# Due dates shifted per stage and chunk in a planned four-layer kernel on one core

## The chip, the cores and the metric

The kernel runs on one core of a Trainium2 chip. The metric is the device time of one execution in microseconds (us). The engines are named as in the profile: PE (matmuls), PEld (its weight loads), DVE (VectorE), ACT (ScalarE), POOL (GpSimd) and SP (SyncE, which issues the DMAs).

## The reference, cut to what matters

The input is x with 32 images of 128 channels and 56 x 56 points, float32. Four layers follow each other; each works on the group-normalised x and adds its result to x:

```python
x = x + dynamic_conv(_gn(x))      # layer 0: pooled softmax mixes 4 channel matrices; then silu of 3 dilated depthwise convs
x = x + spline(_gn(x))            # layer 1: cubic B-spline with 10 coefficients, point by point
x = x + linear_attention(_gn(x))  # layer 2: 8 heads on 8x8 pooled cells, then a depthwise 3x3
x = x + mamba(_gn(x))             # layer 3: layer norm, gated selective scan over all 3136 points
```

The scan of layer 3 is the heart of it. It has 256 inner channels with 16 states each, and runs along the points:

```python
dA  = exp(delta[..., None] * A)
dBu = delta[..., None] * B_ssm[:, :, None, :] * xc[..., None]
h   = dA_t * h + dBu_t                 # step by step over the points
y   = einsum('bdn,bn->bd', h, C_t)
out = einsum('bld,cd->blc', (y + xc * D) * silu(z), out_proj_w)
```

## The kernel before, in words

An image's 3136 points are cut into 7 chunks of 448. The scan of one chunk is 16 steps. In each step ACT makes the decays (two `da` activations), PE spreads the B rows (`pb`), DVE multiplies (`db`) and runs the scan instruction (`h`), POOL multiplies by the C rows (`hc`), and every other step PE sums the products (`y`). At the end of a chunk DVE multiplies by the gate (`sz`), PE projects (`mm<-sz,outT`), DVE adds to the image (`xt<-xt,mm`), and SP stores.

Three images are in work at the same time. While image b is scanned ("scan"), the inputs of its next chunk are made ("next", and "gate" for the silu gate), layers 1 and 2 and the norm weights of image b+1 are worked through ("rest"), and layer 0 of image b+2 ("conv"). `images` writes all this down for 6 images, and a hardware loop runs that block 5 times; a block before it makes the first two images ready, and a block behind it scans the last two images.

The order is not the written one. The class `Plan` records each operation as a `Work` with an engine, what it reads and writes, a cost from a formula (`price`), and a step: the number of the scan step beside which it was written. `order` then gives each work a due date, from the back: its step times `STEP` (4.0), or earlier where something that needs it is due earlier. To that date the table `LEAD` adds a shift. `attempt` is a list scheduler: engine by engine it takes the ready work that can start first by the costs, and among those the one due first, from the steps at most `WINDOW` (10) ahead of the first one not done. It also chooses the buffers (five of tag "v", four of PSUM "mm", three `da`, three `h`). `issue` then writes the instructions in that order. So every instruction carries the line of `issue`, L500 in the profile, and the tiles' names tell it apart.

The shift is looked up under two names:

```python
for w in self.works:
    chunk = w.step % (NCH * STEPS) // STEPS
    w.due += LEAD.get(w.what, 0.0) + LEAD.get(f"{w.what.split()[0]} {chunk}", 0.0)
```

`w.what` is the kind of work: stage, engine, the tile written and the first one read ("next scalar cen mm"). The second name is the stage and the chunk, 0 to 6, of the image that is being scanned ("rest 5"). Before the change the table has no entry of the second form, so that look-up always gives 0. A positive shift makes a work due later. What decides between two ready works on an engine is

```python
late = at + 0.3 * (w.table is not None and w.table != table)
key = (max(late, free[e]), w.due, i)
```

so a date counts only between works that could start at the same time, above all on an engine that has a queue of ready works. Nothing in the plan forbids a change of activation tables on ACT (exp, ln and silu need different ones); a load stands in the program wherever two neighbours differ.

Of the kernel before, what the change touches and what calls it, by code (L numbers as in the profile page):

```python
# [79 lines left out]
READY = 12  # L80

LEAD = {
    "conv gpsimd att att": -19.5,
    "conv gpsimd attb att": 18,
    "conv gpsimd attr att": -19,
    "conv gpsimd pooled mv": 6.5,
    "conv gpsimd pooled pooled": -7.5,
    "conv gpsimd rs ve": 6,
    "conv gpsimd xt xt": 3,
    "conv scalar aggT mm": 4.5,  # L90
    "conv scalar att att": -10.5,
    "conv scalar g mm": -34.5,
    "conv scalar part dwT": -66,
    "conv scalar vv mv": -34.5,
    "conv sync padded yc": 15,
    "conv sync stack padded": 38,
    "conv sync xt x_dram": 30,
    "conv tensor mm aggT": 24,
    "conv tensor mm dsT": 6,
    "conv tensor mm fc1T": -24.5,  # L100
    "conv tensor mm gmat": -10.5,
    "conv tensor mm ident": 4.5,
    "conv vector aggb aggb": 30.5,
    "conv vector aggb attb": -12.5,
    "conv vector att mm": -6,
    "conv vector hid mm": -18.5,
    "conv vector mv st": -69.5,
    "conv vector mx att": -22,
    "conv vector mx mx": 43.5,
    "conv vector st xt": -123.5,  # L110
    "conv vector ve mm": -20.5,
    "gate scalar sz mm": -3.5,
    "gate tensor mm wzT": 17.5,
    "next gpsimd delta delta": -15,
    "next gpsimd du delta": -186,
    "next gpsimd rstd cen": -157,
    "next gpsimd xn rstd": -26.5,
    "next scalar cen mm": -444.5,
    "next scalar dbl mm": 1,
    "next scalar delta mm": -30.5,  # L120
    "next scalar du du": 2.5,
    "next scalar du mm": -75,
    "next scalar rstd mm": 9.5,
    "next scalar rstd rstd": 12,
    "next scalar sq mm": -29,
    "next scalar xc mm": 47.5,
    "next sync flat delta": 11,
    "next sync flat du": 27,
    "next tensor mm ctr": -0.5,
    "next tensor mm dtT": -134.5,  # L130
    "next tensor mm jmat": -152.5,
    "next tensor mm winT": -6,
    "rest gpsimd ab ve": -84,
    "rest gpsimd ind xt": 5,
    "rest gpsimd mcell mcell": 20.5,
    "rest gpsimd rs ve": -13.5,
    "rest gpsimd rstd cen": 8.5,
    "rest gpsimd xn": 39,
    "rest gpsimd xt xt": 2.5,
    "rest scalar cen mm": 1.5,  # L140
    "rest scalar ctr cen": 61,
    "rest scalar hats hats": -32,
    "rest scalar hats mm": 3.5,
    "rest scalar rstd mm": 2.5,
    "rest scalar rstd rstd": 18.5,
    "rest scalar sq mm": -10,
    "rest scalar top ab": 1,
    "rest scalar vv mv": 10.5,
    "rest scalar ws mm": -38,
    "rest scalar ws ws": 26.5,  # L150
    "rest sync padded yc": -35.5,
    "rest sync stack padded": -36,
    "rest tensor mm ctr": -24,
    "rest tensor mm gmat": -31,
    "rest tensor mm ident": 6.5,
    "rest tensor mm jmat": 2.5,
    "rest tensor mm wpT": -36.5,
    "rest tensor mm wqT": -4.5,
    "rest tensor mm ws": 10.5,
    "rest tensor mm wspl": -147.5,  # L160
    "rest tensor mm wv": -13.5,
    "rest vector ab mg": 31.5,
    "rest vector ab rs": -29,
    "rest vector bia bia": -8,
    "rest vector bia kneg": -15.5,
    "rest vector cb mm": -12,
    "rest vector cube sq": -6.5,
    "rest vector kb mm": -3,
    "rest vector mcell mg": -45,
    "rest vector mg mm": 16.5,  # L170
    "rest vector mv st": -13.5,
    "rest vector nm": 26,
    "rest vector nm mg": 39.5,
    "rest vector rden mm": 4.5,
    "rest vector rden rden": -3,
    "rest vector st xt": 82.5,
    "rest vector ve mm": -113.5,
    "rest vector ws mm": 12,
    "rest vector xt mm": 14,
    "rest vector xt xt": -4.5,  # L180
    "scan gpsimd hc h": 1.5,
    "scan gpsimd last h": -47.5,
    "scan gpsimd rep last": 83.5,
    "scan scalar cb mm": -114,
    "scan scalar da rep": 9,
    "scan sync out_dram xt": 7,
    "scan sync rep flat": -19.5,
    "scan tensor mm outT": 22,
    "scan tensor mm sel": 7.5,
    "scan tensor pb sel": -45,  # L190
    "scan tensor y ddiag": 12,
    "scan tensor y ids": 4.5,
    "scan vector db rep": -7.5,
    "scan vector h da": 42.5,
    "scan vector sz sz": 193,
    "scan vector xt xt": 40.5,
    "sync rep flat": 8,
}

GN_EPS = 1e-5  # L200
# [1383 lines left out]
```

## Time and profile before

| | us |
|---|---|
| median of 3 runs | 14355.79 (14342.31 to 14364.07) |
| the profiled execution | 14350.93 |
| its span, first to last instruction | 14349.1 |
| first scan instruction after the start | 425.5 |
| one turn of the loop, 6 images | 2613.6 to 2621.4 |
| an image in the middle of a turn | 428.5 to 431.9 |
| first image of a turn | 448.9 to 454.3 |
| the block behind the loop, 2 images | 822.0 |

The turns and images are measured between the starts of DVE's scan instructions: 16 in a chunk, 112 in an image. A chunk of a middle image takes, from chunk 0 to chunk 6, about 59, 62, 67.5, 67, 56, 59 and 60 us. At the end of a turn all engines run dry and start again, with about 12 us more in the last chunk and 15 us more in the first one; in the 14 us around one such end (5640 to 5654 us) PE's granted clock is 0.51 of full speed.

In the profile's tables a row of a stretch has the span, then for each engine its busy time and the number of its instructions in brackets, PE's granted clock, the share that the DMA engines were busy, and GB/s. A row of waits names the waiting engine and tile, the engine and tile that ended the wait, the sum in us, how often, and the longest. A row of a group has its count, the busy time, the mean duration in ns, and the idle time ahead of it.

### The profile page before, as it was taken

The numbers are of one execution on the slowest core, as the hardware profiler recorded it, in microseconds if no ns is written. First come the engines' busy times: TensorE is split into PE (matmuls) and PEld (weight loads), VectorE is DVE, ScalarE is ACT, GpSimd is POOL, SyncE is SP. The second block draws the span as 40 slices with busy tenths as digits, with TensorE's granted clock in tenths as the row PEclk, the third lists the DMA queues.
The fourth block names the chain that finished last, engine by engine and source line by source line (L and its number), as shares of the span: only waits on it lengthen the run. The fifth ranks groups of instructions, "written<-read, shape, count | busy, mean of one in ns | idle before, by whom it ended". The sixth has DMA issues, their size and how long they took to land. (4 is left out here: it accounts for less than half of the span.)

```text
span 14349.1 us, 308089 instructions
## 1 busy us (share of the span) xinstructions
PE 12973.7 (90%) x122016; PEld 4333.4 (30%) x122016; DVE 12525.2 (87%) x10849; ACT 12711.8 (89%) x19296; POOL 11326.6 (79%) x10150
## 2 busy tenths in 40 slices
PE   7899999989999998999999999999998999999886
PEld 2223333323333332333233333333332333332221
DVE  1799989889888898898999888998988898989899
ACT  4899999989999998999999889999998899999886
POOL 2688888878788887888888878888887788888777
PEclk8999999999999999999999999999999999999998
DMA  5566566556665565665665655666655656656443
GB/s 128 121 140 141 134 151 140 131 128 140 139 146 134 135 140 131 145 141 131 141 141 136 145 126 134 138 141 143 147 133 127 138 134 150 141 129 143 109 107 74
DMA packets 1135727, 1927.31 MB, mean 134 GB/s; under 512 B 96434, under 2 KB 1133874, under 8 KB 1134260
## 3 DMA queue, kind: packets, MB, share of 16 engines
q1 hardware_dynamic: 1134260, 1907.39, 58.3%
q8 instruction: 965, 15.81, 0.5%
q14 instruction: 502, 4.11, 0.1%
HBM read 1541.47 MB, written 365.54 MB: 133 GB/s over the span
## 5 line engine op out<-in xcount | busy, mean ns | idle before, releaser
L500 POOL TENSOR_TENSOR hc<-h,cb 128x896 f32<-128x896 f32 x3584 | 7541.5, 2107 | 497.0 <-DVE h L500 240.6
L500 DVE TENSOR_TENSOR_SCAN h<-da,db 128x904 f32<-128x904 f32 x3584 | 7288.5, 2034 | 548.4 <-ACT da L500 236.9
L500 ACT ACTIVATE da<-rep,alog 128x448 f32<-128x448 f32 x7168 | 4477.1, 674 | 989.7 <-DVE h L500 765.1
L500 DVE TENSOR_TENSOR db<-rep,pb 128x904 f32<-128x904 f32 x3584 | 3944.5, 1101 | 352.7 <-POOL rep L500 82.4
L500 ACT ACT_TABLE_LOAD x1849 | 2372.3, 1283 | 50.1 <-DVE h L500 13.8
L500 PE MATMUL y<-hc,ids 128*32 128x448 f32 x14336 | 2023.7, 552 | 344.2 <-POOL hc L500 340.1
L500 PE MATMUL pb<-dbl,sel 128*32 128x452 f32 x14336 | 1825.9, 571 | 340.3 <-DVE db L500 308.5
L500 POOL TENSOR_TENSOR xt<-xt,v 128x448 f32<-128x448 f32 x1344 | 1538.6, 1146 | 465.0 <-ACT v L500 325.3
L500 PE MATMUL mm<-stack,dsT 96*32 96x448 f32 x16128 | 1819.2, 559 | 69.9 <-ACT wide L500 33.8
L500 POOL COPY last<-h 128x2 f32<-128x2 f32 x3072 | 572.7, 187 | 1628.3 <-DVE h L500 1511.1
L500 PE MATMUL mm<-xn,winT 128*32 128x448 f32 x14336 | 1588.4, 559 | 71.6 <-POOL xn L500 55.8
L500 ACT ACTIVATE wide<-mm,bia 128x448 f32<-128x448 f32 x2688 | 1557.8, 657 | 20.3 <-PE mm L500 18.3
L500 ACT ACTIVATE wide<-wide,one,scl 128x1344 f32<-128x1344 f32 x896 | 1377.6, 1537 | 7.7
L500 PE MATMUL mm<-wide,wspl 128*32 128x448 f32 x12544 | 1307.7, 560 | 56.2 <-DVE xt L500 27.9
L500 PE MATMUL mm<-xt,ident 128*32 128x448 f32 x8960 | 1082.6, 544 | 89.7 <-ACT cb L500 28.4
L500 PEld LDWEIGHTS y<-hc,ids 128*32 128x32 f32 x14336 | 533.9, 111 | 1439.0 <-POOL hc L500 689.5
L500 PE MATMUL mm<-dbl,sel 128*32 128x448 f32 x7168 | 865.4, 543 | 67.1 <-ACT yc L500 38.5
L500 PEld LDWEIGHTS mm<-stack,dsT 96*32 96x32 f32 x16128 | 547.6, 111 | 1113.6 <-issue 874.8
L500 PEld LDWEIGHTS pb<-dbl,sel 128*32 128x32 f32 x14336 | 393.7, 110 | 1439.9 <-DVE db L500 1124.5
L500 PEld LDWEIGHTS mm<-xn,winT 128*32 128x32 f32 x14336 | 474.9, 112 | 994.2 <-issue 778.1
L500 PEld LDWEIGHTS mm<-wide,wspl 128*32 128x32 f32 x12544 | 434.5, 114 | 897.0 <-issue 700.4
L500 DVE BATCH_NORM_STATS2 st<-xt 128x6 f32<-128x448 f32 x896 | 541.0, 613 | 135.3 <-POOL xt L500 131.9
(178 smaller groups left out, 13564.0 us busy)
## 6 DMA issues: line engine op xcount, KB each, us to landing
rep<-flat SPq DMA_DIRECT2D x1792, 448.0 KB, 8.3
stack<-padded SPq DMA_DIRECT2D x2016, 246.5 KB, 6.5
stack<-padded SPq DMA_DIRECT2D x672, 228.5 KB, 4.3
flat<-delta SPq DMA_DIRECT2D x224, 448.0 KB, 2.6
flat<-du SPq DMA_DIRECT2D x224, 448.0 KB, 2.8
padded<-yc SPq DMA_DIRECT2D x224, 244.0 KB, 2.2
padded<-yc SPq DMA_DIRECT2D x256, 199.5 KB, 3.4
xt<-x_dram SPq DMA_DIRECT2D x224, 224.0 KB, 9.3
```

Of the source, the lines that this page charges most:

```text
L500: call.func(*map(self.bind, call.args), **{k: self.bind(v) for k, v in call.keywords.items()})
```

## The change

The table `LEAD` is replaced. It gets 28 entries of the form stage and chunk, and nearly all entries by kind of work have other values; a few kinds lose their entry or get one. Nothing else in the program differs, neither the look-up nor any operation. Cut to its core:

```diff
 LEAD = {
-    "conv gpsimd att att": -19.5,
...
-    "conv scalar part dwT": -66,
...
+    "conv 1": -1,
+    "conv 2": 1.5,
+    "conv 5": -10.5,
+    "conv 6": -3,
+    "conv gpsimd att att": -11.5,
...
-    "gate scalar sz mm": -3.5,
-    "gate tensor mm wzT": 17.5,
+    "gate 0": 9.5,
+    "gate 1": 2.5,
+    "gate 2": 16,
+    "gate 3": 15,
+    "gate 4": 24.5,
+    "gate 5": 201,
+    "gate 6": 26.5,
+    "gate scalar sz mm": -4.5,
+    "gate tensor mm wzT": 13.5,
...
-    "next gpsimd du delta": -186,
-    "next scalar cen mm": -444.5,
-    "next tensor mm dtT": -134.5,
+    "next 0": -1,
+    "next 1": -1.5,
+    "next 2": -1,
+    "next 3": -1,
+    "next 4": 1,
+    "next 5": 4.5,
+    "next 6": -2.5,
+    "next gpsimd du delta": -164,
+    "next scalar cen mm": -438.5,
+    "next tensor mm dtT": -44.5,
...
+    "rest 1": 0.5,
+    "rest 2": 0.5,
+    "rest 3": -2.5,
+    "rest 4": 4.5,
+    "rest 5": 11.5,
+    "rest 6": 21.5,
...
-    "scan scalar cb mm": -114,
-    "scan vector sz sz": 193,
+    "scan 0": 0.5,
+    "scan 2": 3.5,
+    "scan 4": 5,
+    "scan 5": 20.5,
+    "scan scalar cb mm": -140.5,
+    "scan vector sz sz": 159,
...
 }
```

The dates decide the order, and the order decides the buffers and the places of ACT's table loads; so in the built program, by a comparison engine by engine, a good part of the instructions of the loop stand at another place in their queue or use another buffer of the same tag, and ACT has 349 table loads in a turn of the loop where it had 347. The block before the loop and the one behind it keep their number of them.

More of the change, by code (lines that the diff above doesn't have):

```diff
@@ L82 @@
 LEAD = {
-    "conv gpsimd att att": -19.5,
[L84 to L92, printed above, removed]
-    "conv scalar part dwT": -66,
[L94 to L97, printed above, removed]
@@ L98 @@
-    "conv tensor mm aggT": 24,
[L99 to L111, printed above, removed]
-    "gate scalar sz mm": -3.5,
@@ L113 @@
-    "gate tensor mm wzT": 17.5,
-    "next gpsimd delta delta": -15,
-    "next gpsimd du delta": -186,
-    "next gpsimd rstd cen": -157,
-    "next gpsimd xn rstd": -26.5,
-    "next scalar cen mm": -444.5,
[L119 to L127, printed above, removed]
@@ L128 @@
-    "next sync flat du": 27,
-    "next tensor mm ctr": -0.5,
-    "next tensor mm dtT": -134.5,
[L131 to L142, printed above, removed]
+    "conv 1": -1,
@@ new lines @@
+    "conv 2": 1.5,
+    "conv 5": -10.5,
+    "conv 6": -3,
+    "conv gpsimd att att": -11.5,
+    "conv gpsimd attb att": 10,
+    "conv gpsimd attr att": -9.5,
+    "conv gpsimd pooled mv": -47,
+    "conv gpsimd pooled pooled": -10.5,
+    "conv gpsimd rs ve": -25,
+    "conv scalar aggT mm": 26,
+    "conv scalar att att": 14.5,
+    "conv scalar g mm": -161,
+    "conv scalar vv mv": -11.5,
+    "conv scalar yc mm": 5.5,
+    "conv sync padded yc": 6,
+    "conv sync stack padded": -14.5,
@@ new lines @@
+    "conv sync xt x_dram": 11,
+    "conv tensor mm aggT": 24,
+    "conv tensor mm dsT": 5.5,
+    "conv tensor mm fc1T": -0.5,
+    "conv tensor mm gmat": 5,
+    "conv tensor mm hid": 11,
+    "conv tensor mm ident": 17,
+    "conv vector aggb aggb": 43.5,
+    "conv vector aggb attb": 56,
+    "conv vector att mm": 10,
+    "conv vector hid mm": 0.5,
+    "conv vector mv st": 12.5,
+    "conv vector mx att": 31,
+    "conv vector mx mx": 41.5,
+    "conv vector st xt": 37,
+    "conv vector ve mm": 15,
@@ new lines @@
+    "gate 0": 9.5,
[14 more added lines that the diff above has]
+    "next 6": -2.5,
+    "next gpsimd delta delta": -29,
+    "next gpsimd du delta": -164,
+    "next gpsimd rstd cen": -130,
+    "next gpsimd xn rstd": -34.5,
+    "next gpsimd xn xn": -19.5,
@@ new lines @@
+    "next scalar cen mm": -438.5,
+    "next scalar dbl mm": -73.5,
+    "next scalar delta mm": -67,
+    "next scalar du du": -8,
+    "next scalar du mm": -26,
+    "next scalar rstd mm": 12.5,
+    "next scalar rstd rstd": 11,
+    "next scalar sq mm": -17.5,
+    "next scalar xc mm": 5,
+    "next sync flat delta": -16.5,
+    "next sync flat du": -46,
+    "next tensor mm dtT": -44.5,
+    "next tensor mm jmat": -106.5,
+    "next tensor mm winT": -6.5,
+    "next tensor mm xprojT": 1,
+    "rest 1": 0.5,
@@ L143 @@
+    "rest 2": 0.5,
[3 more added lines that the diff above has]
+    "rest 6": 21.5,
+    "rest gpsimd ab ve": -55,
+    "rest gpsimd ind xt": 27.5,
+    "rest gpsimd mcell mcell": 11.5,
+    "rest gpsimd rs ve": -46,
+    "rest gpsimd rstd cen": -48,
+    "rest gpsimd xn": -19.5,
+    "rest gpsimd xn rstd": 2,
+    "rest gpsimd xt xt": 3,
+    "rest scalar cen mm": 17.5,
+    "rest scalar ctr cen": -33.5,
+    "rest scalar hats hats": -6.5,
     "rest scalar hats mm": 3.5,
-    "rest scalar rstd mm": 2.5,
@@ L145 @@
-    "rest scalar rstd rstd": 18.5,
+    "rest scalar rstd mm": -42.5,
+    "rest scalar rstd rstd": 11.5,
     "rest scalar sq mm": -10,
[L147 to L183, printed above, removed]
-    "scan scalar cb mm": -114,
[L185 to L194, printed above, removed]
-    "scan vector sz sz": 193,
-    "scan vector xt xt": 40.5,
-    "sync rep flat": 8,
+    "rest scalar top ab": -28,
+    "rest scalar vv mv": -21,
+    "rest scalar ws mm": -59,
+    "rest scalar ws ws": -19.5,
+    "rest scalar yc mm": -28.5,
+    "rest sync padded yc": -3.5,
+    "rest sync stack padded": -7,
+    "rest tensor mm ctr": -4.5,
@@ new lines @@
+    "rest tensor mm gmat": -103.5,
+    "rest tensor mm ident": 6,
+    "rest tensor mm jmat": 16.5,
+    "rest tensor mm wpT": -5.5,
+    "rest tensor mm wqT": 0.5,
+    "rest tensor mm ws": 5,
+    "rest tensor mm wspl": -201,
+    "rest tensor mm wv": -5,
+    "rest vector ab mg": 11.5,
+    "rest vector bia bia": 1,
+    "rest vector bia kneg": -55,
+    "rest vector cb mm": 49,
+    "rest vector cube sq": 135.5,
+    "rest vector kb mm": -6,
+    "rest vector mcell mg": 7.5,
+    "rest vector mv st": 17.5,
@@ new lines @@
+    "rest vector nm": 24.5,
+    "rest vector nm mg": -8,
+    "rest vector rden mm": 5,
+    "rest vector rden rden": -4.5,
+    "rest vector scl mm": 27,
+    "rest vector st xt": 8.5,
+    "rest vector ve mm": 6,
+    "rest vector ws mm": -59,
+    "rest vector xt xt": 1,
+    "scan 0": 0.5,
+    "scan 2": 3.5,
+    "scan 4": 5,
+    "scan 5": 20.5,
+    "scan gpsimd hc h": 0.5,
+    "scan gpsimd last h": -6.5,
+    "scan gpsimd rep": 5,
+    "scan gpsimd rep last": 3.5,
+    "scan scalar cb mm": -140.5,
@@ L198 @@
+    "scan scalar da rep": 8.5,
+    "scan sync out_dram xt": -38,
+    "scan sync rep flat": 2.5,
+    "scan tensor mm outT": 21.5,
+    "scan tensor mm sel": 8,
+    "scan tensor pb sel": -74.5,
+    "scan tensor y ddiag": 10.5,
+    "scan tensor y ids": 5.5,
+    "scan vector db rep": 31,
+    "scan vector h da": 54,
+    "scan vector sz sz": 159,
+    "scan vector xt xt": 1.5,
+    "sync rep flat": -17.5,
 }
```

## The prediction

> **What bounds the kernel now.** First the page's first part. All four engines are busy for most of the span, so no single engine is "the" bound, and the share over the whole span does not say where a shift of work would pay.
>
> ```profile
> span 14349.1 us, 308089 instructions
> PE 12973.7 (90%) x122016; PEld 4333.4 (30%) x122016; DVE 12525.2 (87%) x10849; ACT 12711.8 (89%) x19296; POOL 11326.6 (79%) x10150
> ```
>
> The work repeats per image (7 chunks of 16 scan steps), so I cut one image out of the middle of the second turn of the loop, at the starts of the first scan of each chunk, and asked for the busy time of each engine in the seven stretches.
>
> ```profile
> core 0: us, PE busy (x) PEld busy (x) DVE busy (x) ACT busy (x) POOL busy (x), PEclk, DMA share, GB/s
> 4356.50:4415.80 59.30, 52.93 (x508) 18.98 (x508) 55.97 (x55) 58.81 (x95) 51.32 (x53) 1.00 0.39 95
> 4415.80:4477.40 61.60, 56.94 (x545) 17.33 (x543) 54.62 (x42) 58.53 (x90) 52.38 (x48) 0.94 0.72 160
> 4477.40:4544.90 67.50, 62.91 (x649) 21.09 (x645) 56.61 (x46) 67.23 (x103) 59.43 (x54) 1.00 0.61 136
> 4544.90:4612.20 67.30, 65.52 (x663) 22.95 (x656) 56.52 (x52) 64.09 (x100) 55.27 (x53) 1.00 0.60 134
> 4612.20:4668.30 56.10, 54.71 (x458) 19.21 (x456) 53.93 (x44) 46.54 (x70) 44.10 (x42) 1.00 0.69 163
> 4668.30:4726.80 58.50, 52.42 (x476) 17.31 (x472) 56.90 (x51) 47.69 (x72) 45.42 (x42) 0.97 0.73 161
> 4726.80:4786.80 60.00, 53.01 (x546) 16.61 (x534) 55.56 (x51) 53.51 (x80) 45.91 (x31) 0.97 0.56 132
> ```
>
> The reader is to see two halves. In chunks 0 to 3 (the first four rows, 255.7 us) ACT is busy for 58.81 + 58.53 + 67.23 + 64.09 = 248.7 us, 97%; in chunk 3 PE is as tight, 65.52 of 67.30. In chunks 4 to 6 (174.6 us) ACT has 26.9 us to spare and DVE is the bound: 53.93 + 56.90 + 55.56 = 166.4 us, 95%. A perfect balance of the two halves would shorten the image; work that stays in its half shortens it only by what the bound engine waits. So next the waits of ACT in the first half and of DVE in the second.
>
> ```profile
> ACT da L500 <- issue: 2.0, 1, 2.0
> ACT v L500 <- PE mm L500: 2.0, 1, 2.0
> ACT da L500 <- DVE h L500: 0.8, 3, 0.4
> ACT wide L500 <- PE mm L500: 0.7, 1, 0.7
> ACT du L500 <- PE mm L500: 0.5, 1, 0.5
> ```
>
> ```profile
> DVE mg L500 <- PE mm L500: 2.1, 1, 2.1
> DVE h L500 <- ACT da L500: 0.2, 1, 0.2
> DVE db L500 <- DVE h L500: 0.2, 1, 0.2
> ```
>
> That is 6.0 us of waits for ACT and 2.5 us for DVE, 8.5 us in an image of 430.3 us. The rest of DVE's idle time, 174.6 - 166.4 - 2.5 = 5.7 us over 144 instructions, is 40 ns between neighbours and does not depend on the order.
>
> **The change, part by part.** It edits no instruction's shape; it only re-dates the work, so every instruction is still there and the question is what passes what. I counted in the order of the two built programs, engine by engine, taking the scan's own instruction as a ruler (h on DVE, hc on POOL, da on ACT, pb on PE), and priced what crosses a chunk's border with rows of the page (busy time over count).
>
> (1) Where the work lies. POOL's and DVE's instructions stand in the same chunks as before except for single ones (DVE's sum in chunks 4 to 6 is the same). On average an instruction moves by 0.3 of a scan step, the gate's two activations by 0.9. So the second half keeps its bound: nothing on DVE leaves it.
>
> (2) Table loads on ACT, 1283 ns each:
>
> ```profile
> L500 ACT ACT_TABLE_LOAD x1849 | 2372.3, 1283 | 50.1 <-DVE h L500 13.8
> ```
>
> A middle image has 58 of them before and after. By chunk they go from 5, 5, 7, 9, 10, 11, 11 to 5, 5, 7, 8, 7, 13, 13. One load leaves the half that ACT bounds: -1.28 us in each of the loop's 30 images (in the two images behind the loop the first half keeps its number), 30 x 1.283 = -38.5 us. The other three leave chunk 4, where ACT has 9.6 us to spare, and land in chunks 5 and 6, where it has 10.8 and 6.5 us: nothing, as long as that idle time is there; without it 4 x 1.283 = 5.1 us an image.
>
> (3) Two more table loads in each turn of the loop (347 to 349), 5 x 2 x 1.283 = 12.8 us of ACT. They stand in the last image's chunk 6, where ACT waits for the turn to end anyway:
>
> ```profile
> 5654.15 2.34 ACT L500 ACTIVATE da<-rep,alog 128x448 f32<-128x448 f32 x4 [19.66 <-PEq L1492]
> ```
>
> Those 19.66 us cover them: 0; without that cover +12.8.
>
> (4) On PE, chunk 1 loses about 3 us to its neighbours, and chunks 2 and 3 gain about 2.1 us each. In chunk 2: one group of y (2023.7 us / 1792 = 1.13), one of mm<-dbl,sel (865.4 / 896 = 0.97), one of mm<-xc,xprojT (407.2 / 448 = 0.91), less one of mm<-stack,dsT (1819.2 / 2016 = 0.90). In chunk 3: xprojT 0.91, dsT 0.90, the transpose of pooled cells 0.30. Chunk 2 has 67.50 - 62.91 = 4.6 us of idle PE, which covers it. Chunk 3 has 67.30 - 65.52 = 1.8 us: 2.1 - 1.8 = 0.3 us an image is not covered, +9 us over 30. Without the cover it is +2.1 an image.
>
> (5) A burst on ACT in chunk 4. Between two da instructions after step 2 there now stand an ln block and a silu block with three table loads, some 8.0 us by the rows, where the longest in that chunk was under 5. Behind it on ACT is the next da, behind that DVE's h, then hc and y. DVE lives from the da buffers, of which there are three; a step takes 174.6 / 48 = 3.64 us, so two in store last 7.3 us. Between 0 and 8.0 - 7.3 = 0.7 us an image, 0 to +21 us; below nothing it can't go, since DVE's waits for da in that half are 0.2 us now. I take 0, as the buffers are nearly always full there.
>
> (6) All the rest: waits between engines, redrawn. The trace of before can't show them. From below: all 8.5 us go, 30 x 8.5 = -255. From above: the nearest rows are the same waits, doubled: +255. POOL, PE and SP queues move too: on SP about one issue in nine moves by a few places, the loads of x not at all; its DMAs fill 58.3% of 16 engines' span, and none of the waits shown above is one for a landing. The new dates shift whole stages against each other per chunk, that is, they can act just where an engine waits; but the order they start from has only 2% left on the bound engines. I take -1 us an image, an eighth of the wait that there is, -30 us.
>
> [...]
>
> The sum: -38.5 + 0 + 9 + 0 - 30 = -60 us on the profiled execution's own 14350.9 us (span 14349.1, 1.8 us around it), 14,291; the median of the three runs is 4.9 us above that execution, so I say 14,290.
>
> **The rivals.**
> - PE in chunk 3 becomes the bound (slower). Mechanism: (4), with the 1.8 us of idle PE not usable because it lies between dependent groups, as the same idle time does now. It decides as soon as PE has less idle time in chunk 3 than what it was given; ACT's table load then saves nothing, as PE ends last. Behind the added groups on PE stands the next pb, for which DVE's db and h wait. Price: 2.1 x 30 = +63 us, 14,414; with chunk 2's 2.1 as well +126, 14,477. For it: PE at 97% in chunk 3, and chunk 3 among the two longest. Against it: ACT, not PE, ends last in chunk 2.
> - The waits on the bound engines mostly go (much faster). All 8.5 us and the table load: 30 x (8.5 + 1.28) = -293 us, 14,058; half of it 14,204. For it: shifts per chunk aim at single waits of 2 us. Against it: 2.0 of them is named "issue", which no order moves.
> - The change doesn't do what it says: the shifts are large in number ("gate 5" by 201) but the buffers, not the dates, hold the work where it is, as the average move of 0.3 of a step says. Then 14,351 within 0.2%, which is about what a measurement of this kernel can tell from no change (29 us; its three runs span 22).
>
> **How the numbers follow.** Forecast (faster by 0.2 to 1%): 0.40, its own range 14,210 to 14,325. Much faster: 0.12. No difference: 0.18. PE in chunk 3, or a like new wait in the first half, slower: 0.30. Faster 0.52, within 0.2% 0.18, slower 0.30. The range for 8 in 10 leaves out the far half of the much faster case and the far end of the slower one: 14,150 to 14,460.
>
> **What would show it.** In the profile after, the image cut at its chunks: chunk 3 at 66 to 66.5 us with eight or nine loads; ACT still at 97% in chunks 0 to 3, DVE at 95 to 96% in chunks 4 to 6; ACT_TABLE_LOAD x1859 and 2385 us busy. PE over 66.5 us busy in chunk 3 with ACT idle there is the first rival. "DVE h <- ACT da" in chunk 4 above 0.2 us shows (5) wrong. An image under 425 us, or DVE's or ACT's work moved to the other half, shows that (1) misread the order.

## The result, and the profile after

The changed kernel is slower: 14415.47 us, the median of 6 runs (14406.85 to 14426.70), beside 14356.58 us for the kernel before (6 runs, 14342.31 to 14376.82). The ratio is 1.0041, with a 95% interval of 1.0028 to 1.0054. The profiled execution took 14413.91 us with a span of 14412.1 us, 63.0 us more than the span before. Predicted were 14,290 us, so the sign was wrong; the time lies inside the stated range.

The first lines of the page of after answer to those shown of before. PE is busy for 114 us more although it runs the same 122016 instructions; DVE is where it was, and ACT has 30 us more, 13 of them table loads.

```profile
span 14412.1 us, 307635 instructions
...
PE 13087.9 (91%) x122016; PEld 4467.9 (31%) x122016; DVE 12522.5 (87%) x10849; ACT 12741.6 (88%) x19306; POOL 11317.6 (79%) x10150
```

The same cut, an image in the middle of the second turn of after, at the starts of the first scan of its seven chunks (here and in the cut of before, 0.3 us ahead of these starts; columns as before: the stretch, its length, busy time of each engine, PE's granted clock, DMA share, GB/s):

```profile
4381.80:4442.60 60.80, 52.47 (x488) 17.51 (x488) 56.33 (x56) 59.45 (x94) 51.51 (x53) 0.97 0.37 89
4442.60:4499.30 56.70, 50.82 (x504) 16.54 (x504) 53.79 (x41) 55.95 (x85) 50.01 (x46) 1.00 0.80 176
4499.30:4569.70 70.40, 67.02 (x692) 22.89 (x696) 56.68 (x46) 69.89 (x108) 61.26 (x56) 1.00 0.61 135
4569.70:4637.30 67.60, 66.30 (x663) 23.61 (x659) 56.40 (x52) 62.67 (x100) 55.03 (x53) 1.00 0.56 126
4637.30:4695.90 58.60, 56.93 (x448) 19.85 (x444) 53.82 (x43) 44.99 (x69) 44.23 (x42) 0.91 0.69 158
4695.90:4755.90 60.00, 54.80 (x480) 18.48 (x475) 57.48 (x52) 48.29 (x72) 45.13 (x42) 0.93 0.70 156
4755.90:4815.80 59.90, 55.38 (x564) 24.36 (x556) 55.62 (x51) 56.05 (x83) 46.18 (x31) 0.96 0.58 135
```

The reader is to see two things. The first half has only changed its shares: chunk 1 gave 4.9 us away, chunk 0 and chunk 2 took 1.5 and 2.9 us, and the sum is 255.5 us where it was 255.7. The second half grew from 174.6 to 178.5 us though DVE, its bound, is busy for 166.9 us as against 166.4. In chunk 4 PE has 10 records fewer than before and is busy 2.2 us longer, and its granted clock went from 1.00 to 0.91.

One image may be an exception, so here are the means of the 20 images in the middles of the five turns, from the starts of the scan instructions, with the time at half clock from the trace's record of the granted clock (which has 1.00 and 0.50 and nothing between; a stretch at 0.50 counts for the chunk in which it begins):

| chunk | 0 | 1 | 2 | 3 | 4 | 5 | 6 | image |
|---|---|---|---|---|---|---|---|---|
| before, us | 59.76 | 61.09 | 67.54 | 67.30 | 56.12 | 59.06 | 60.26 | 431.14 |
| after, us | 60.92 | 56.67 | 70.43 | 67.59 | 58.36 | 60.30 | 59.90 | 434.16 |
| before, us at half clock | 1.19 | 5.12 | 0 | 0 | 1.54 | 5.12 | 4.95 | 17.9 |
| after, us at half clock | 3.41 | 0 | 0 | 0 | 9.39 | 7.51 | 4.10 | 24.4 |

Over all 30 images of the loop the mean image went from 436.38 to 438.40 us: +0.06 in chunks 0 to 3 and +1.97 in chunks 4 to 6. That is 30 x 2.02 = +60.7 us; the start has +5.2 us (first scan at 430.7 us) and the block behind the loop -2.9 us (819.1), together the 63.0 us. One of before's 20 middle images took 435.5 us, above the 428.5 to 431.9 us of the table ahead; it is in these means.

The longest waits of ACT in the first half of that image of after, and those of DVE in the second:

```profile
ACT da L530 <- DVE h L530: 2.9, 3, 2.0
ACT da L530 <- DVE ve L530: 1.0, 1, 1.0
ACT cb L530 <- POOL hc L530: 0.9, 1, 0.9
```

```profile
DVE xt L530 <- PE mm L530: 2.2, 1, 2.2
DVE mg L530 <- PE mm L530: 1.6, 1, 1.6
DVE cb L530 <- PE mm L530: 0.7, 1, 0.7
```

Both engines wait for others than before. New for DVE is the first row: the sum of the image and the projection, `xt<-xt,mm`, waits 2.2 us for PE. In the 20 images this wait in chunk 4 went from 0 to 1.92 us, and DVE's whole idle time there from 2.28 to 4.59.

Now chunk 4 from close by, PE's rows and that one of DVE, first of after, then of before (start, duration, engine, operation, what it writes and reads, shape, count, and in brackets the idle time just before and what ended it):

```profile
4644.25 0.94 PE L530 MATMUL mm<-sz,outT 128*32 128x448 f32 x8
...
4647.76 1.57 PE L530 MATMUL pb<-dbl,sel 128*32 128x452 f32 x8 [0.62 <-DVE db L530]
...
4649.98 3.57 PE L530 MATMUL mm<-kb,wide 64*128 64x1 f32 x16 [0.66 <-DVE kb L530]
...
4653.48 1.72 PE L530 MATMUL y<-hc,ids 128*32 128x448 f32 x8
...
4655.14 2.88 PE L530 MATMUL mm<-xt,wide 128*64 128x392 f32 x4
...
4657.94 1.07 PE L530 MATMUL mm<-sz,outT 128*32 128x448 f32 x8
...
4659.09 0.62 DVE L530 TENSOR_TENSOR xt<-xt,mm 128x448 f32<-128x448 f32 x1 [2.15 <-PE mm L530]
```

```profile
4619.15 1.71 PE L500 MATMUL mm<-sz,outT 128*32 128x448 f32 x16
...
4622.74 0.96 PE L500 MATMUL pb<-dbl,sel 128*32 128x452 f32 x8
4623.53 0.94 PE L500 MATMUL y<-hc,ids 128*32 128x448 f32 x8
...
4625.20 1.94 PE L500 MATMUL mm<-kb,wide 64*128 64x1 f32 x16 [0.74 <-DVE kb L500]
...
4627.07 1.53 PE L500 MATMUL mm<-xt,wide 128*64 128x392 f32 x4
```

This is layer 2's attention for the next image. Eight pairs of matmuls with 2 columns (bv, nm; two records for each matmul) give kb, DVE copies it, and eight matmuls with 1 column (kb, 16 records) follow. Before, a full y group stood between the pb group and kb. After, y comes behind kb, and a second thing moved: the two projection groups `mm<-sz,outT` of the chunk, which before follow each other (the 16 records at 4619.15), are nearly 14 us apart, the first at 4644.25, ahead of the small matmuls, the second at 4657.94. The record of the clock has 0.50 from 4647.98 to 4658.22 us, and the durations go with it: pb 1.57 for 0.96, y 1.72 for 0.94, `mm<-xt,wide` 2.88 for 1.53, kb 3.57 for 1.94. And yet PE is never idle for longer than 0.66 us here. In the record of the clock all 20 middle images of after have such a stretch, 10.2 us long in 15 of them and 6.8 us in 5; of before, 8 of 20, 3.4 us in 7 and 6.8 us in one.

So two theories stood. **C, the clock**: the small matmuls and the short idle times around them leave PE so little to do that the granted clock falls; PE then comes late for DVE, in the half that DVE bounds. **O, the order**: the second projection group is simply behind too much on PE, and the clock only goes along with it.

### The profile page after: what moved, and what is told of

Its sections match the earlier page's. It is cut to its first block, busy times and chain, and to the rows that moved or that the text cites. A ratio compares the mean times of both kernels' runs of the same rounds, so it can differ in the third digit from the quotient of the medians.

```text
span 14412.1 us, 307635 instructions
## 1 busy us (share of the span) xinstructions
PE 13087.9 (91%) x122016; PEld 4467.9 (31%) x122016; DVE 12522.5 (87%) x10849; ACT 12741.6 (88%) x19306; POOL 11317.6 (79%) x10150
## 5 line engine op out<-in xcount | busy, mean ns | idle before, releaser
L530 ACT ACT_TABLE_LOAD x1859 | 2385.1, 1283 | 70.8 <-DVE h L530 35.0
L530 PE MATMUL mm<-xt,ident 128*32 128x448 f32 x8960 | 1050.2, 544 | 89.3 <-ACT v L530 25.4
L530 PEld LDWEIGHTS mm<-stack,dsT 96*32 96x32 f32 x16128 | 581.6, 111 | 1051.7 <-issue 798.3
L530 PEld LDWEIGHTS mm<-xn,winT 128*32 128x32 f32 x14336 | 509.8, 113 | 934.3 <-issue 717.4
L530 DVE TENSOR_TENSOR xt<-xt,mm 128x448 f32<-128x448 f32 x448 | 274.0, 612 | 503.1 <-PE mm L530 503.1
```

Source lines behind the costliest of these rows:

```text
L530: call.func(*map(self.bind, call.args), **{k: self.bind(v) for k, v in call.keywords.items()})
```

## The experiments

Each ratio is to the kernel before, run again beside the experiments (medians 14361.03 us for e1 to e4, 14363.04 for e5 to e8, 14357.09 for e9 to e11). The changed kernel was not run again beside them; a gain against its 14415.47 us carries the few us by which these medians differ.

**e1: the small matmuls made wide, in after.** They compute the same columns again, so that each has 64 columns; the order of all instructions stays.

```diff
-        pb = psum(2 * HEADS, P2)
+        pb = psum(FILL * HEADS, P2)
...
-                nc.tensor.matmul(pb[:, 2 * h : 2 * h + 2], k[:, hp], bv1[:], start=True, stop=False)
+                nc.tensor.matmul(at_h, k[:, hp], bv1[:].unsqueeze(1).to_broadcast([P, FILL // 2, 2]), start=True, stop=False)
...
-                pd[:, h : h + 1], qT[:, h * P : (h + 1) * P], kb[:, 2 * h + 1 : 2 * h + 2], start=True, stop=True
+                pd[:, FILL * h : FILL * h + FILL], qT[:, h * P : (h + 1) * P], kb[:, 2 * h + 1 : 2 * h + 2].to_broadcast([P2, FILL]), start=True, stop=True
```

> The changed kernel, same order on every engine; only the 24 tiny matmuls of the linear attention that stand in chunk 4 (free size 1 or 2) get a free size of 64, by repeating their columns; what the rest reads is unchanged. Theory C (clock): these matmuls leave PE so idle that its granted clock falls to half for 9.4 us of chunk 4 in a middle image (1.5 before the change), PE then ends late and DVE's xt<-xt,mm waits 1.9 us for it. By C the half clock in chunk 4 falls to under 2 us, chunk 4 goes from 58.4 back to 56 to 56.5 us and the kernel from 14415 to about 14350 (30 images x 2.2 us). Theory O (order): the wait comes from the place of mm<-sz,outT behind the attention's matmuls, at whatever clock. By O chunk 4 stays at 58 us and the kernel within 15 us of 14415.

Measured: 14376.72 us, ratio 1.0013 [1.0004, 1.0022]. In the middle images chunk 4 takes 57.73 us and is at half clock for 5.97 us instead of 9.39. More work on PE in the same order made the kernel 39 us faster than after, which speaks for the clock; but the result lies between what the two theories said, and most of the half clock stayed, so the width of these matmuls isn't the whole of it.

**e2: the second projection group put back behind the first, in after.** In chunk 4 alone, on PE alone.

```diff
+            out.remove(b)
+            out.insert(out.index(a) + 1, b)
```

> The changed kernel with one thing moved: in chunk 4, the second group of mm<-sz,outT on PE goes to the place right behind the first one, 13 us earlier, ahead of the attention's tiny matmuls; all other instructions stay in their order. Theory O: DVE's xt<-xt,mm in chunk 4 no longer waits (1.9 us to under 0.2 in a middle image), chunk 4 goes to 56.5 us and the kernel to about 14358. Theory C: the half clock (9.4 us in chunk 4) stays and PE stays late for the next thing that DVE or POOL needs; the kernel gains less than 20 us.

Measured: 14357.18 us, 0.9999 [0.9990, 1.0008]. The wait of `xt<-xt,mm` in chunk 4 is gone (1.92 to 0 us), but DVE now sits idle for 2.28 us ahead of its db there, 1.50 of them waiting for pb, where it was 0.92 and none for pb: of 1.92 us won, 1.36 came back one instruction later. Chunk 4 takes 57.59 us and is at half clock for 7.68. In the loop the mean image is 2.4 us shorter than after's, 0.8 in chunk 4 and 0.4 to 0.6 each in chunks 5, 6 and 0. So the order takes back 58 of the 59 us, and O is alive: what stands between the first group and the second decides how long DVE waits. But chunk 4, for which O said 56.5 us, is still 1.5 us longer than before's, and PE's half clock is still there.

**e3 and e4: one part of the change alone.** e3 is before's entries by kind with the 28 new entries by stage and chunk; e4 is after without those 28.

```diff
 LEAD = {
+    "conv 1": -1,
...
+    "gate 5": 201,
...
+    "scan 5": 20.5,
```

> The kernel before with the 28 entries by stage and chunk added and its own entries by kind kept. Theory P (the two sets of entries only fit together): the program has 482 table loads where before has 464, of them 3 more in a turn of the loop, and the time is 0.2 to 1% above before, 14385 to 14500. If the entries by chunk alone make the loss, it is at 14415 like the changed kernel. If they are a gain that the entries by kind lose, it is under 14340.

> The changed kernel without the 28 entries by stage and chunk. Theory P: slower than the changed kernel, 14430 to 14550. If the entries by kind alone make the loss, it is at 14415. If the entries by chunk make it, it is at before's 14357 or under.

Measured: 14968.15 us, 1.0426 [1.0410, 1.0442], and 15016.30 us, 1.0460 [1.0444, 1.0476]. Both are far above what any theory had said. A middle image takes 446.0 and 452.6 us, with 36.9 and 33.4 us at half clock, and there are 1959 and 1951 table loads where after has 1859. The two sets of dates belong together, so taking one out doesn't tell what the other adds, and these two runs say nothing on C and O.

**e5: y ahead of kb, in after.** This one group of PE goes back ahead of the eight kb matmuls in chunk 4, as it stands in before. Everything else is after.

```diff
+            y = next(i for i in order[at[z]:] if works[i].what == "scan tensor y ids")
...
+            out.remove(y)
+            out.insert(out.index(a), y)
```

> The changed kernel with one thing moved: in chunk 4 of each image in the loop, the group of y that stands on PE right behind the eight mm<-kb matmuls goes ahead of them, where PE waits 1.2 us for DVE's kb copy and the products are ready. Theory C2: it is this gap, next to matmuls that hardly use PE, that lets the granted clock fall; with y in the gap the half clock in chunk 4 goes from 9.4 us to under 4 in a middle image, the kb matmuls take 1.9 us again in place of 3.5, and PE is in time for mm<-sz,outT although its place is kept: DVE's wait of 1.9 us goes, and the kernel is at 14350 to 14375. Theory O (the place of outT alone): the clock is beside the point, the wait at xt stays over 1.2 us and the kernel is at 14395 to 14415.

Measured: 14329.98 us, 0.9975 [0.9966, 0.9984]: not only the whole loss of 59 us is gone, the kernel is now 33 us below before, and 20 us below what C2 had said. The same place of e5:

```profile
4192.82 0.97 PE L552 MATMUL pb<-dbl,sel 128*32 128x452 f32 x8 [0.62 <-DVE db L552]
4193.61 0.94 PE L552 MATMUL y<-hc,ids 128*32 128x448 f32 x8
...
4195.05 1.94 PE L552 MATMUL mm<-kb,wide 64*128 64x1 f32 x16 [0.51 <-DVE kb L552]
4196.92 1.53 PE L552 MATMUL mm<-xt,wide 128*64 128x392 f32 x4
4198.38 0.96 PE L552 MATMUL mm<-sz,outT 128*32 128x448 f32 x8
```

The idle times are nearly those of after (0.62 and 0.51 us for 0.62 and 0.66), the durations are those of before (kb 1.94 us, `mm<-xt,wide` 1.53, y 0.94). The projection groups are still apart, but the second comes 5.6 us behind pb's start instead of 10.2, and `xt<-xt,mm` waits 0.23 us in the mean. Chunk 4 takes 56.32 us, with 2.56 us at half clock; 13 of 20 images have none there.

The other images of e5 tell the clock from the order. The order is one and the same in all turns of the loop, and yet in 4 of the 20 images the clock falls just ahead of the kb matmuls, for 10.2 us. Chunk 4 takes 58.3 to 58.6 us in these four and 55.7 to 56.1 us in the 16 others, in which kb runs at full speed. Here are two images from the same place of the loop, in its second and third turn:

```profile
5044.09:5102.38 58.29, 57.05 (x445) 20.08 (x444) 53.81 (x42) 45.05 (x68) 43.87 (x42) 0.91 0.68 161
7657.34:7713.06 55.72, 52.75 (x448) 17.78 (x444) 53.57 (x42) 44.62 (x68) 44.03 (x42) 1.00 0.71 167
```

With the same instructions in the same order, DVE is busy for as long, and at the granted clock of 0.91 PE takes 4.3 us more and the chunk 2.6 us more.

**e6: y ahead of kb, and the projection groups together** (the edits of e2 and e5).

> Both moves of PE's order in chunk 4: y ahead of the kb matmuls and the second mm<-sz,outT behind the first. If the slow PE after the kb matmuls is what was left in chunk 4 with outT moved (57.6 us where before has 56.1), chunk 4 goes to 56.0 to 56.5 and the kernel to 14310 to 14335, under before. If clock and place are two names for one loss, it is at 14357 like with outT alone.

Measured: 14321.16 us, 0.9972 [0.9962, 0.9982], the same as e5 within the intervals, and in the range that was expected if the slow PE was what e2 had left. Chunk 4 takes 55.88 us. With PE at speed, the split of the projection costs next to nothing, so O alone, at whatever clock, is no cause.

**e7: the reverse, in before.** In before, y is moved behind kb in chunk 4, in 5 of the 6 images of a turn (in the other one something needs it earlier). The projection groups stay together.

```diff
+            y = [i for i in order[: at[a]] if works[i].what == "scan tensor y ids"][-1]
...
+            out.remove(y)
+            out.insert(out.index(z) + 1, y)
```

> The kernel before with the opposite move: in chunk 4 of five of the six images of a turn, the y that stands ahead of the kb matmuls goes right behind them. Theory C2: the half clock in chunk 4 rises from 1.5 us to 6 to 10 in those images, chunk 4 gets 1 to 2 us longer there, the kernel is at 14385 to 14415. Theory O: outT keeps its early place in this kernel, so it stays within 15 us of before, 14361.

Measured: 14418.82 us, 1.0041 [1.0027, 1.0055], the same loss as the whole change, and a little more than C2 had said. Chunk 4 of a middle image:

```profile
4202.20:4260.90 58.70, 56.83 (x458) 20.75 (x456) 54.08 (x44) 46.56 (x70) 44.22 (x42) 0.94 0.67 156
```

Against before's row of the same chunk (56.10 us, PE 54.71, the same 458 records, clock 1.00) PE is busy 2.1 us longer, and the chunk is 2.6 us longer. All 20 images have 6.8 us at half clock here. With the projection together, DVE's db pays (3.16 us idle ahead of it in the mean, 2.53 of them waiting for pb), not `xt`. So this one group's place is enough for the loss, and the split isn't needed for it.

**e8: the small matmuls made wide, in before** (the edit of e1).

> The kernel before with the tiny matmuls of the linear attention at a free size of 64. In the kernel before, they run at full clock already, with 1.5 us of half clock in chunk 4: by C and C2 up to 0.5 us an image to win, 14345 to 14361; by O nothing. Over 14375 would say that a wider matmul costs time here, which would take some of the force out of the same edit on the changed kernel.

Measured: 14339.79 us, 0.9985 [0.9976, 0.9994], somewhat better than expected. Chunk 4 has no half clock left in any of the 20 images (1.54 us before).

**e9: y stays late, and the pb group ahead of kb is issued twice, in after.** The second issue writes the same values again; it is 0.96 us of PE work that nobody needs. This tells the clock from the queue: if y's place matters only because y is late, more work on PE ahead of it should make it worse.

```diff
-                for call in works[i].calls:
+                for call in works[i].calls * (1 + (i in again)):
```

> The changed kernel, y left behind the kb matmuls, with redundant work in the gap: in chunk 4 of each image in the loop, the pb group that stands ahead of the kb matmuls is issued twice (0.96 us more of PE, the same values written again). If it is the clock that carries the loss (theory C2), any full matmul in the gap helps: the kb matmuls take under 2.5 us (3.5 in the changed kernel), half clock in chunk 4 falls from 9.4 to under 5 us, and the kernel is at 14335 to 14380 although PE has more to do. If it is the late y that carries it, by holding POOL's buffers, the kernel is at 14415 or above it by up to 30 us.

Measured: 14342.87 us, 0.9991 [0.9982, 1.0000]. Adding useless work took 72 us off after's time. Chunk 4 takes 56.75 us with 3.41 us at half clock, and `xt` waits 0.44 us. The kb matmuls, 512 records in the whole run, by groups of before, after and e9 (busy us, mean ns of one, idle time ahead):

```profile
L500 PE MATMUL mm<-kb,wide 64*128 64x1 f32 x512 | 67.7, 259 | 22.3 <-DVE kb L500 22.3
```

```profile
L530 PE MATMUL mm<-kb,wide 64*128 64x1 f32 x512 | 108.7, 338 | 26.6 <-DVE kb L530 26.6
```

```profile
L544 PE MATMUL mm<-kb,wide 64*128 64x1 f32 x512 | 80.2, 283 | 8.9 <-DVE kb L544 8.7
```

The 41 us that these 512 records gained in after are mostly gone in e9, with kb at the same place in the order; the second pb fills most of the wait ahead of it (26.6 us of idle time to 8.9). So of the 85 us between e5 and after, 72 come back with y behind kb as before: that goes with the clock (9.39 us of half clock in chunk 4 of after, 3.41 in e9), and y's lateness in the queue can't be the bulk of it. The rest, 13 us by the medians and 23 by the ratios, may be y's own lateness or the half clock that is left; that stays open. The gains of e1, e2, e9 and e5 (39, 58, 72 and 85 us) don't add up, which fits one chain that each of them breaks at another link: the small matmuls, the group that comes late for DVE, the clock, the order that lets the clock fall.

**e10 and e11: y ahead of kb and the small matmuls wide, in after; e11 with the projection groups together as well.**

> The changed kernel with y ahead of the kb matmuls, and the tiny matmuls at a free size of 64. In four of the twenty middle images of the profile with y ahead the clock still falls for 10.2 us in chunk 4. If the wide tiny matmuls hold it there, 14310 to 14325, under both kernels; if the clock has no more to give, 14330 within 10 us.

> The same with the second mm<-sz,outT moved behind the first as well. With both moves only 0.5 us of half clock is left in chunk 4, so the wide tiny matmuls can win less than 5 us there: 14310 to 14325. More than that would come from other chunks.

Measured: 14307.22 us, 0.9966 [0.9952, 0.9979], and 14306.48 us, 0.9965 [0.9951, 0.9978]. Both are some 3 us below the range that was expected. They beat both kernels, before by some 50 us and after by 108. Chunk 4 of e10 takes 55.80 us, with 1.02 us at half clock, and the whole run has 874 us at half clock, where before has 973 and after 1219. e11 adds nothing to e10: the split of the projection is harmless once the clock holds. e8 is the old order with wide small matmuls, at 0.9985 [0.9976, 0.9994]; beside it the new order with y moved is some 0.2% faster, though the intervals just touch. So with the clock nearly held in chunk 4 in both, the new dates may be worth a part of what was predicted; that is not shown.

**Where the falls stand.** In the records of the clock, all 167 falls of before lie whole steps of 3413.3 ns apart, within 1 ns, and so do all 201 of after. So where the ends of these steps lie beside the kb matmuls, which differs from image to image, has to be looked at together with the order. At such ends up to 1.2 us behind the start of kb, reached at full clock, the clock fell in 31 of 31 middle images in which y stands behind kb (after, e2, e7), and in 0 of 49 in which y (before, e5, e6) or the second pb (e9) stands ahead of it. This is what a full group at y's place did here; later ends don't tell the orders apart so well, as before's own falls stand 1.5 to 1.7 us behind the start of kb. But in 15 of the 20 images of after the clock falls 2.0 to 2.7 us ahead of kb, before the place that y left; the pb group, at 1.57 us, is slow already. What left the stretch ahead of that place is the second projection group: where it is back (e2, e6), none of 14 images with such an end there loses the clock, and none of 13 does where the small matmuls are wide (e1, e10). So two full groups left this part of PE's order in after, and by these counts the places of both matter. In e5's profile no step ends at such a place; a part of what e5 won can lie in where its steps happen to end, and no run separates that.

## Why the prediction was wrong

Its steps, in its own order.

- **(1) held.** No work changed halves: DVE's busy time in chunks 4 to 6 is 166.9 us (166.4), the image's first half 255.5 us (255.7).
- **(2) failed in what it was worth.** The load did leave chunk 3: the first half has 25 loads in the trace (26 or 27 before, as one stands at the border to chunk 4), and ACT_TABLE_LOAD is x1859 with 2385.1 us as the step said. But ACT's busy time in the first half fell by 0.7 us an image (248.7 to 248.0) and its idle time rose by as much (6.95 to 7.59), so the first half as a whole, -38.5 + 9 by steps (2) and (4), measured 30 x 0.06 = +2 us. The idle time rose in chunk 3, from 3.23 to 4.93 us. There PE is busy for 66.30 of 67.60 us, so the reading from these rows is that the load left a chunk in which ACT no longer ended last. No run tried that by itself.
- **(3) held.** The two more loads a turn lie in the wait at the turn's end, which is as long as it was:

```profile
L530 ACT ACT_TABLE_LOAD x1859 | 2385.1, 1283 | 70.8 <-DVE h L530 35.0
```

```profile
5689.54 2.35 ACT L530 ACTIVATE da<-rep,alog 128x448 f32<-128x448 f32 x4 [19.72 <-PEq L1522]
```

- **(4) came out in its number for chunk 3, but not in its working.** The chunk went from 67.30 to 67.59 us in the mean, the +0.3 us that the step priced. But PE's busy time rose by 0.8 us there (65.52 to 66.30, with 663 records in both rows) and not by 2.1, and its idle time was not used up (1.8 to 1.3 us), so that the two numbers meet is luck. In chunk 2 PE took 4.1 us more instead of 2.1 (62.91 to 67.02) and the chunk grew by 2.9 us; ACT took 2.7 us more there as well, from chunk 1, which became 4.4 us shorter in the mean.
- **(5) held.** DVE's idle time ahead of h, which reads da, is 1.49 us in chunk 4 of a middle image in the mean, where it was 1.48.
- **(6) is the step that failed.** "Waits between engines, redrawn", taken at -30 us, measured +59 us in the second half (30 x 1.97; an image has +1.73 in chunk 4, +0.99 in chunk 5 and -0.75 in chunk 6, and no run takes the last two apart). The size lies within the step's bounds of ±255 us. What was wrong is the assumption under it: that matmuls keep their durations from the rows of before whatever stands between them. PE's time for the same work was not a constant of the kernel: a y group of 0.94 us, moved behind the kb matmuls, took 1.72 us with its neighbours slowed alike, and DVE, which had 2.3 us of idle time in chunk 4, had 4.6.

The prediction's sum has no term for the granted clock. Chunk 1, where PE lost work by step (4), lost all its half clock (5.12 us to none), though its PE is idle for longer than before (56.70 - 50.82 = 5.9 us, 4.7 before); why was not tried. Chunk 4, where the amount of PE's work hardly changed (458 records, now 448), went from 1.54 to 9.39. Little idle time of PE stands ahead of these falls: in the 15 of the 20 middle images of after in which the clock falls ahead of kb, PE is idle for at most 0.62 us at a time in the 7 us ahead of the fall, in the other five for at most 1.26 us. The stretches at half clock there, 6.8 and 10.2 us, are two and three of the steps of 3413.3 ns.

Its sum has one slip, on which nothing hangs: 14,291 us is for an execution like the profiled one, and a median 4.9 us above that would be 14,296 us, not 14,290.

The time of 14,414 us that the first rival named is what was measured, but by another mechanism, so that is luck too. That rival had PE as the bound of chunk 3; chunk 3 grew by 0.3 us, and the loss came in chunk 4, from PE's speed. The rival "does not do what it says" is out: the order moved by much, and e3 and e4 show that dates of this size move the time by over 4%.

## What to carry to other kernels

A change of order has to be priced twice: once with the durations of the old trace, and once for what it does to the durations, above all where small matmuls and short idle times of PE meet (here kb went from 259 to 338 ns). Look at PE's granted clock stretch by stretch in the bound engine's stage, not at the mean (0.966 to 0.958 here, and 1.00 to 0.91 in chunk 4 of the images shown), and ask of each stretch with little PE work which full group stands in it; if one leaves, the clock may fall there, as in e7, where chunk 4 had 6.8 us at half clock for before's 1.54. And where matmuls have one or two columns, widening them to 64 cost PE little here (a kb matmul took 275 ns in e8, 259 in before) and helped to hold the clock (in chunk 4 no half clock in e8, 1.54 us in before).

## What the runs showed of the hardware

- In 15 of the 20 middle images of after the granted clock fell to 0.50 with no idle time of PE over 0.62 us in the 7 us ahead of the fall, between the 2-column matmuls and the 1-column ones. With one more full group of 0.94 to 0.96 us ahead of the 1-column ones, useful (e5) or not (e9), 13 (e5) and 11 (e9) of the 20 images kept the full clock at this place, where after has none. What PE's activity must be for it was not measured, and the fall is not the same in every image of one run: in e5 13 of 20 have none in chunk 4, 3 have 3.4 us and 4 have 10.2.
- With 64 columns a kb matmul took 275 ns in the mean (e10), with one column 259 ns (before); a bv matmul took 224 ns (e10) with 64 columns and 200 ns with two (before). In after, where chunk 4 of a middle image is at half clock for 9.39 us, the 1-column ones took 338 ns in the mean.
- Useless work on PE made the changed kernel faster: e9 stands at 0.9991 [0.9982, 1.0000] of before, after at 1.0041 [1.0028, 1.0054].
